# Base rows of a mixture-of-experts output: stored whole and overwritten, or added and scattered tile by tile

## The chip, the cores and the metric

The kernel runs on one core of one Trainium2 chip. The metric is the device time of one launch in microseconds; three runs of the kernel before gave a median of 1457.72 us. Times inside the kernel are from one profiled execution and count from the start of its span.

## What is computed

The input is 2048 tokens (2 x 1024) of 256 numbers. Four layers are applied one after another, each as `x = x + ffn(cond(x))`. The change lies in the end of the last one. Its `cond` part is a mixture of experts with a shared part: every token goes to two of eight experts, and the sum of shared and routed results is divided by three. Call its result h. Its `ffn` part is this, with 16 experts and room for 160 tokens in each:

```python
probs = softmax(h @ Wg)                          # 2048 x 16
top1_val, top1_idx = probs.max(-1), probs.argmax(-1)
masked = where(top1_idx[None, :] == arange(16)[:, None], top1_val[None, :], -inf)
vals, idx = top_k(masked, 160)                   # the best 160 tokens of each expert
y = gelu(h[idx] @ W1 + b1) @ W2 + b2
ffn = h.at[idx].set(y)                           # tokens without a place keep h
out = x + ffn
```

So a row of the output is x + y where the token has a place in its expert, and x + h, called the base row here, where it has none.

## The kernel before

Tokens are cut into 16 tiles of 128 (NT = 16, P = 128) and into four blocks of 512 (NB = 4). `k.Xt` holds x with one token in each of 128 partitions, 16 x 256 numbers wide; `k.Ht` (its tile is named ACC in the profile) holds h in the same way; `k.XT` and `k.HT` hold x and h with channels in the partitions, as TensorE needs them. SyncE (SP) issues the loads of weights and rows, ScalarE (ACT) a few stores, GpSimd (POOL) all transfers that go by a list of row numbers. A scheduler orders the instructions of each engine by their dependencies and by hints (`_behind` is such a hint: an order without a wait).

Layer 3 begins in `_cond_moe` (L1927) with the layer's `Last` object as `next`. Three blocks of the shared part are computed while the routing is worked out, then 39 expert slots, then the fourth block of the shared part. During this fourth block `Tokens.add` (L1656) loads two expert rows for each token (yt, 256 KB for a tile, five buffers) and VectorE adds them into Ht with their gates (L1665, two instructions for a tile). `_back` (L1584) transposes each finished tile into HT: TensorE writes ps_bk, ScalarE copies it (L1591).

The final routing, `Last.chunk` (L2206), works by block and is hooked into the same stretch:

- `logits` (L2216): ScalarE's queue stores h into the left half of the rows of a DRAM buffer hx (L2217); POOL adds h to x in place (L2219, 128x1024), so that Xt then holds the base rows; TensorE multiplies by Wg (l3f_pt), ScalarE copies.
- `top` (L2230): a transpose (l3f_pl), then VectorE takes the maximum (l3f_m, L2236), the difference (l3f_lg, L2238) and the choice (l3f_eq, L2241); ScalarE takes the exponential (L2242).
- `rows` (L2250): one-hot rows and the split gate value (l3f_z), multiplied by TensorE into l3f_ps (L2266); POOL keeps running counts (L2271 to L2273).
- `beats` (L2284): compares tokens with tokens to get each token's rank in its expert.

`Last.begin` (L2173) had, earlier, stored the old x into the right half of the rows of hx (L2190). `Last.finish` (L2323) runs what is left of the four blocks, issues the four stores of the base rows into the output (L2339 to L2343, 512 KB each, from SP), the 16 loads of b2 (into XT, which is free by then) and the first weights, and turns ranks into row numbers: `numbers` (L2396) makes, for each of 16 slots of 128 ranks and for 4 groups of 4 x 32 ranks, the list `src` of rows to gather and the list `dst` of rows to write. An empty place gets a number beyond the last row, and the transfer skips it (`bounds_check`). The b2 rows of the groups (b2g) go into the last four tiles of Ht (L2390).

`Last.run` (L2409) takes the 20 pieces in the order slot, slot, slot, slot, group and so on. Five gathers are begun ahead. For each piece TensorE transposes the gathered rows (ps_cm), VectorE copies them (xsT, L2484), TensorE multiplies by W1 (l3f_ph, or l3f_gh for a group), ScalarE applies gelu, TensorE multiplies by W2 (l3f_po), VectorE adds b2 and then x (ys, L2426 and L2427), and POOL scatters the 128 rows into the output (L2428). `_after(k, s, self.outs)` (L2433) makes the scatters wait until the four stores of base rows have landed. Then POOL issues the gather of the piece five places later (L2492).

Of the kernel before, what the change touches and what calls it, by code (L numbers as in the profile page):

```python
# [9 lines left out]
F32 = mybir.dt.float32  # L10
I32 = mybir.dt.int32
U32 = mybir.dt.uint32
# [1914 lines left out]
def _cond_moe(k, name, wr, bias, W1, W3, W2, nf, hold, R1, R2, gate_mult, final, lead, most, next=None):  # L1927

    nc, A, XT, HT, Xt, Ht = k.nc, k.A, k.XT, k.HT, k.Xt, k.Ht
    rp, pool, psum = k.rp, k.pool, k.psum  # L1930
    E, T, NS = 8, P, 39
    base = 0 if next else 8192
    w, rb = k.small[wr], k.small[bias]
    sets = []
    for i in range(4):
        r = k.ring.take(1, hold).rearrange("p (n c f) -> p n c f", n=2, f=D)
        sets.append([(r[:, 0], A[R1]), (r[:, 1], A[R2])])
    def routing(lead_):
        s = rp.tile([P, NT, E], F32, name=name + "_s", tag="s")
        _logits(k, psum, rp, XT, w, E, name, s, AF.Sigmoid, k.small[wr, "b"])  # L1940
        sel = rp.tile([P, NT, E], F32, name=name + "_sel", tag="lg")
        nc.vector.tensor_tensor(sel, s, _bc(rb, 1, [P, NT, E]), ALU.add)
        _, ixf = _top(nc, rp, sel, E, name)
        _name_rows(k, k.Xr, ixf, base)
        oh = [_one_hot(k, rp, ixf, n, E, name + "_oh%d" % n, "oh%d" % n) for n in range(2)]
        M = rp.tile([P, NT, E], F32, name=name + "_M", tag="M")
        nc.vector.tensor_add(M, oh[0], oh[1])
        cum = _running(k, rp, M, E, name)
        yield
        pos, eid, of, used = _route(k, rp, psum, M, cum, E, T, NS, len(sets), name)  # L1950
        rows = [_rows_of(k, rp, oh[n], pos, E, name + "_rows%d" % n, "rows%d" % n) for n in range(2)]
        k.x.begin()
        lead_.sends = k.x.paced(k.Xr, rows)

        nc.vector.tensor_mul(M, M, s)
        den = rp.tile([P, NT], F32, name=name + "_den", tag="den")
        nc.vector.tensor_reduce(den, M, AX.X, ALU.add)
        big = rp.tile([P, NT], F32, name=name + "_big", tag="big")
        nc.vector.tensor_single_scalar(big, den, 1e-9, ALU.is_gt)
        nc.vector.tensor_scalar_add(den, den, 1e-9)  # L1960
        nc.vector.reciprocal(den, den)
        nc.vector.tensor_mul(den, den, big)
        nc.vector.tensor_scalar(big, big, -0.5, 0.5, ALU.mult, ALU.add)
        gate = []
        for n in range(2):
            nc.vector.tensor_mul(oh[n], oh[n], s)
            g = rp.tile([P, NT], F32, name=name + "_g%d" % n, tag="g%d" % n)
            nc.vector.tensor_reduce(g, oh[n], AX.X, ALU.add)
            nc.vector.tensor_mul(g, g, den)
            nc.vector.tensor_add(g, g, big)  # L1970
            nc.vector.tensor_scalar_mul(g, g, gate_mult * final)
            gate.append(g)
        lead_.made = gate, eid, of, used

    def shared(tb, hook=None, mid=None, added=lambda: False):
        if nf == 8 and tb == 0:
            po = _shared_first(k, pool, psum, XT, W1, W3, W2, hook)
        else:
            po = _shared(k, pool, psum, XT, tb, W1, W3, W2, nf, hook, mid)
        for i in range(2):  # L1980
            t = tb * 4 + i * 2
            if added():
                nc.vector.scalar_tensor_tensor(Ht[:, t:t + 2, :], po[i], final, Ht[:, t:t + 2, :],
                                               ALU.mult, ALU.add)
            else:
                nc.scalar.activation(Ht[:, t:t + 2, :], po[i], AF.Copy, scale=final)

    lead_ = Lead(k, routing, *((1, 7), 2) if nf == 8 else ((1, 3), 4))
    def hook(f, mul, mm):
        if k.late and lead_.n >= 6:  # L1990
            k.late.pop(0)(mul)
        lead_.hook(f, mul, mm)

    for tb in range(lead):
        shared(tb, hook)
    gate, eid, of, used = lead_.finish()
    k.t.begin()
    by = Slots(k, pool, psum, of, base)

    def slots(lo, hi):  # L2000
        series = Series(k, by, lo, hi)
        for i in range(lo, hi):
            series.slot(i, _gelu_products(k, pool, psum), lambda: _slot_weights(k, eid, i, sets, E))
        series.close()

    used = nc.values_load(used[0:1, 0:1], min_val=0, max_val=NS)
    slots(0, most)
    with k.tc.If(used > most):  # L2008
        slots(most, NS)
    if next:  # L2010
        next.begin()
    c = Tokens(k, pool, psum, gate, Ht, HT, nf, next)
    for tb in range(lead, NB):
        c.there = tb * 4
        shared(tb, c.hook, c.hook, lambda: c.added >= tb * 4 + 4)
    c.there = NT
    k.ring.drop(hold)
    if next:
        next.finish(c)
    else:  # L2020
        c.finish()
# [104 lines left out]
class Last:  # L2126
# [10 lines left out]
    def __init__(self, k):  # L2137
        self.k, E = k, self.E
        rp = k.rp
        self.w = []  # L2140
        self.parts = [self.chunk(q) for q in range(NB)]

        self.plan = {5: [0], 6: [0], 7: [0, 1]}
        k.iota16 = rp.tile([P, CAP], BF16, name="iota16")
        k.nc.vector.tensor_copy(k.iota16, k.iota)
        k.one16 = rp.tile([P, 1], BF16, name="one16")
        k.nc.vector.memset(k.one16, 1.0)
        self.oh = rp.tile([P, NT, E], F32, name="l3f_oh")
        self.val = rp.tile([P, NT], F32, name="l3f_val")

        self.z = rp.tile([P, 4, 2, self.K], BF16, name="l3f_z")
        self.cum = rp.tile([P, NT + 1, E], F32, name="l3f_cum")

        self.acc = rp.tile([P, NT, 7], F32, name="l3f_acc")

        self.ids = rp.tile([P, NT, 2, E], BF16, name="l3f_ids")
        self.down = rp.tile([P, E], F32, name="l3f_down")
        self.th = rp.tile([P, NT], F32, name="l3f_th")
        self.outs = []

    def weights(self, ref=None):

# [10 lines left out]
    def begin(self):  # L2173
# [13 lines left out]
        nc.vector.memset(self.cum[:, 0, :], 0.0)  # L2187
        nc.vector.tensor_scalar(self.down, k.iota[:, 0:self.E], -1.0, float(self.E), ALU.mult, ALU.add)
        nc.vector.tensor_scalar_add(self.th, k.iota[:, 0:NT], 1.0)
        nc.sync.dma_start(k.hx[:, D:2 * D].rearrange("(t p) d -> p t d", p=P), k.Xt)  # L2190
        self.weights()

    def on_act(self, t):

# [11 lines left out]
    def chunk(self, q):  # L2206
# [8 lines left out]

        def logits(mul, mm):  # L2216
            nc.scalar.dma_start(k.hx[cols, 0:D].rearrange("(t p) d -> p t d", p=P), k.Ht[:, ts, :])  # L2217
            x = k.Xt[:, ts, :]
            nc.gpsimd.tensor_tensor(x, x, k.Ht[:, ts, :], ALU.add)  # L2219
            ps = psum.tile([P, P], F32, name="l3f_pt", tag="mm")  # L2220
            for c in range(2):
                for j in range(4):
# [100 lines left out]
    def finish(self, c):  # L2323
# [12 lines left out]
                    ref = p(None, None) or ref  # L2336
        ref = _warm(k, k.psum, ref, 6)
        assert c.put == NT
        for q in range(NB):  # L2339
            i = nc.sync.dma_start(k.out[q * TB:(q + 1) * TB, :].rearrange("(t p) d -> p t d", p=P),  # L2340
                                  k.Xt[:, 4 * q:4 * q + 4, :])
            _behind(k, i, c.load)
            self.outs.append(i.ins.name)  # L2343
        for e in range(E):
            i = nc.sync.dma_start(self.b2[:, e, :], k.A["L3_b2"][e:e + 1].to_broadcast([P, D]))
            _behind(k, i, c.load)
# [36 lines left out]
            _behind(k, i, ref)  # L2383
            ref = i
        self.ref = ref
        s, d, _ = self.numbers(pg, 4, "g")
        self.src, self.dst = ([t[:, i:i + 1] for t, n in ((a, E), (b, 4)) for i in range(n)]
                              for a, b in ((self.src, s), (self.dst, d)))

        self.b2g = k.Ht[:, 12:16, :]  # L2390
        for e in range(E):
            g = e % 4
            nc.sync.dma_start(self.b2g[32 * g:32 * g + 32, e // 4, :],
                              k.A["L3_b2"][e:e + 1].to_broadcast([32, D]))

    def numbers(self, ps, n, name):  # L2396
# [12 lines left out]
    def run(self):  # L2409
# [14 lines left out]
        def end(i, po, b2):  # L2424
            y = pool.tile([P, D], F32, name="ys", bufs=4)
            nc.vector.tensor_tensor(y, po, b2, ALU.add)  # L2426
            nc.vector.tensor_tensor(y, y, at[i][:, D:2 * D], ALU.add)  # L2427
            s = nc.gpsimd.indirect_dma_start(  # L2428
                out=k.out, out_offset=bass.IndirectOffsetOnAxis(ap=self.dst[i], axis=0),
                in_=y, in_offset=None, bounds_check=N - 1, oob_is_err=False)  # L2430
            k.tc.declare_no_dep(s.ins, group="out", reason="rows of their own")
            k.tc.add_to_no_dep_group("out", s.ins)
            _after(k, s, self.outs)  # L2433

        def slot(e, xT):
            W1, W2, _ = self.w[e]
# [45 lines left out]
        for n, i in enumerate(order):  # L2482
            xT = pool.tile([P, 2, P], F32, name="xsT", bufs=3)
            nc.vector.tensor_copy(xT, _channel_major(k, psum, at[i], self.ref))  # L2484
            if i < E:
                end(i, slot(i, xT), self.b2[:, i, :])
            else:
                end(i, group(i - E, xT), self.b2g[:, i - E, :])
                for e in range(4 * (i - E), 4 * (i - E) + 4):
                    k.ring.drop(self.w[e][2])  # L2490
                self.weights()
            fetch(n + 5)  # L2492


def _layer3(k):
# [127 lines left out]
```

## Time and profile before

| | |
|---|---|
| median of three runs | 1457.72 us (1453.08 to 1458.84) |
| profiled execution, own time | 1446.02 us |
| its span | 1444.3 us |
| PE busy | 1396.8 us, 97% of the span |
| VectorE busy | 464.0 us, 32% |
| ScalarE busy | 307.8 us, 21% |
| GpSimd busy | 291.5 us, 20% |
| first and last scatter into the output start | 1356.6 and 1437.2 us |
| granted TensorE clock, mean | 0.988 |

The table is from the page of the profile. A share of the span is a mean over stages that differ: most of the 1444 us are dense matrix products, while the end of layer 3, from about 1281 us on, is a chain of small steps on four engines and then the 20 pieces. PE, DVE, ACT, POOL and SP are TensorE, VectorE, ScalarE, GpSimd and SyncE. L2219 is line 2219 of the kernel before; `out<-in` names the tiles that an instruction writes and reads.

### The profile page before, as it was taken

How to read it: one execution, taken by the hardware profiler on the slowest of the kernel's cores; microseconds unless marked ns; L12 is line 12 of the kernel's file. 1: busy time of each engine (PE TensorE's matmuls, PEld its weight loads, DVE VectorE, ACT ScalarE, POOL GpSimd, SP SyncE). 2: the span in 40 equal slices, each digit the busy share in tenths (PEclk: the TensorE clock that was granted, in tenths of full speed). 3: DMA queues.
4: the chain of work that ended last, by engine and by line, in shares of the span. 5: the costliest groups of instructions: out<-in, count | busy, mean ns of one | idle time of the engine just before them, and what ended most of it. 6: DMA issues, size and time to landing. Idle time of an engine off the chain costs nothing. (4 is left out here: it accounts for less than half of the span.)

```text
span 1444.3 us, 23566 instructions
## 1 busy us (share of the span) xinstructions
PE 1396.8 (97%) x8606; PEld 1002.0 (69%) x8610; DVE 464.0 (32%) x1558; ACT 307.8 (21%) x646; POOL 291.5 (20%) x339
## 2 busy tenths in 40 slices
PE   9999999999999999999999999999999998997897
PEld 4544444545558865565999999999995567874675
DVE  4523322326214442511211111111115513467332
ACT  3222221234112121201111111111112211126221
POOL 0400001200533410331001001001010073433441
PEclk9999999999999999999999999999999999998999
DMA  9879994922314850421335155155507247758470
GB/s 313 297 256 347 358 321 134 275 72 101 125 52 118 260 183 8 188 82 37 113 109 194 48 180 195 46 178 194 193 20 273 93 164 244 225 172 284 123 243 15
DMA packets 176527, 246.78 MB, mean 171 GB/s; under 512 B 16695, under 2 KB 128831, under 8 KB 176400
## 3 DMA queue, kind: packets, MB, share of 16 engines
q1 hardware_dynamic: 154912, 203.18, 43.1%
q0 software_dynamic: 13888, 36.63, 7.2%
q10 hardware_dynamic: 7600, 5.34, 1.1%
q8 instruction: 72, 1.18, 0.3%
q14 instruction: 55, 0.45, 0.1%
HBM read 280.92 MB, written 47.22 MB: 227 GB/s over the span
## 5 line engine op out<-in xcount | busy, mean ns | idle before, releaser
L282 POOL DMA_INDIRECT tbuf<-ys,sdst x108 | 106.3, 984 | 484.8 <-ACT ys L1844 376.6
L1520 PE MATMUL spo<-ring,sa 128*128 128x256 f32 x704 | 164.9, 379 | 0.0
L1520 PEld LDWEIGHTS spo<-ring,sa 128*128 128x128 f32 x704 | 132.5, 190 | 44.6 <-issue 29.1
L1837 DVE TENSOR_TENSOR fa<-fsg,fpu 128x512 f32<-128x512 f32 x72 | 49.5, 688 | 316.2 <-PE fpu L1832 316.2
L1832 PE MATMUL fpg<-xsT,ring 128*128 128x128 f32 x1152 | 140.4, 275 | 0.7 <-issue 0.7
L1543 DVE TENSOR_TENSOR sa<-ssg,spu 128x512 f32<-128x512 f32 x88 | 60.4, 686 | 249.8 <-PE spu L1534 241.2
L1832 PE MATMUL fpu<-xsT,ring 128*128 128x128 f32 x1152 | 140.4, 275 | 0.0
L1832 PEld LDWEIGHTS fpg<-xsT,ring 128*128 128x128 f32 x1152 | 137.0, 192 | 2.7 <-issue 0.9
L1832 PEld LDWEIGHTS fpu<-xsT,ring 128*128 128x128 f32 x1152 | 134.4, 192 | 0.0
L1841 PE MATMUL fpo<-ring,fa 128*128 128x256 f32 x576 | 130.3, 379 | 0.0
L1841 PEld LDWEIGHTS fpo<-ring,fa 128*128 128x128 f32 x576 | 106.7, 190 | 13.0
L1539 ACT ACTIVATE ssg<-spg 128x512 f32<-128x512 f32 x88 | 52.6, 597 | 263.0 <-PE spg L1534 243.6
L1534 PE MATMUL spg<-HT,ring 128*128 128x512 f32 x192 | 92.1, 594 | 2.2 <-issue 1.9
L1534 PE MATMUL spu<-HT,ring 128*128 128x512 f32 x192 | 90.2, 592 | 0.0
L1808 PE MATMUL cph<-xsT,ring 128*128 128x128 f32 x576 | 79.0, 281 | 4.8 <-DMA ring<-in_L_r 2.6
L1836 ACT ACTIVATE fsg<-fpg 128x512 f32<-128x512 f32 x72 | 43.0, 597 | 171.7 <-PE fpg L1832 171.7
L1808 PEld LDWEIGHTS cph<-xsT,ring 128*128 128x128 f32 x576 | 71.2, 194 | 8.8 <-DVE sn L1735 2.8
L1534 PE MATMUL spg<-XT,ring 128*128 128x512 f32 x160 | 75.5, 593 | 1.3 <-PEq L2008 1.2
L1534 PE MATMUL spu<-XT,ring 128*128 128x512 f32 x160 | 75.2, 592 | 0.0
L1815 PE MATMUL cpo<-ring,ch 128*128 128x256 f32 x288 | 73.8, 380 | 0.0
L1534 PEld LDWEIGHTS spu<-HT,ring 128*128 128x128 f32 x192 | 36.3, 190 | 45.0 <-issue 44.2
L1731 DVE COPY xsT<-ps_cm 128x256 f32<-128x256 f32 x132 | 55.1, 418 | 36.7 <-PE ps_cm L365 36.5
(621 smaller groups left out, 1726.1 us busy)
## 6 DMA issues: line engine op xcount, KB each, us to landing
ring<-in_L_w SPq DMA_DIRECT2D x108, 1024.0 KB
ring<-in_L_r SPq DMA_DIRECT2D x72, 512.0 KB
ring<-in_L_r SPq DMA_DIRECT2D x144, 256.0 KB
xs<-xbuf SPq DMA_DIRECT2D x132, 129.0 KB
ring<-in_L_W SPq DMA_DIRECT2D x32, 512.0 KB
yt<-tbuf SPq DMA_DIRECT2D x48, 256.0 KB
XT<-in_L_r SPq DMA_DIRECT2D x16, 512.0 KB
HT<-in_L_r SPq DMA_DIRECT2D x8, 512.0 KB
```

The source lines that it names most:

```text
L282: i = k.nc.gpsimd.indirect_dma_start(out=self.ap, out_offset=bass.IndirectOffsetOnAxis(ap=idx, axis=0), in_=rows, in_offset=None, **end)
L1520: mm = nc.tensor.matmul(po[g // 2][:, g % 2, :], a[:, g * P:(g + 1) * P], W2[:, f, :], start=f == 0 and g % 2 == 0, stop=f == nf - 1, skip ...
L1534: mm = nc.tensor.matmul(ps, W[:, c, f * P:(f + 1) * P], X[:, c, cols], start=c == 0, stop=c == 1)
L1539: k.silu = nc.scalar.activation(sg, pg, AF.Silu)
L1543: mul = nc.vector.tensor_mul(a, sg, pu)
L1731: turned = nc.vector.tensor_copy(xT, _channel_major(k, self.psum, xs, made=made))
L1808: made = [nc.tensor.matmul(ph[:, f, :], R1[:, c, f * P:(f + 1) * P], xT[:, c, :], start=c == 0, stop=c == 1) for f in range(2) for c in ra ...
L1815: made = [nc.tensor.matmul(po, h[:, f, :], R2[:, f, :], start=f == 0, stop=f == 1) for f in range(2)]
L1832: made = [nc.tensor.matmul(ps[:, j, :], W[:, c, (f0 + j) * P:(f0 + j + 1) * P], xT[:, c, :], start=c == 0, stop=c == 1) for ps, W in ((pg, ...
L1836: nc.scalar.activation(sg, pg, AF.Silu)
L1837: nc.vector.tensor_mul(a[:, f0:f0 + 4, :], sg, pu)
L1841: made = [nc.tensor.matmul(po, a[:, f, :], W2[:, f, :], start=f == 0, stop=f == 4 * nh - 1) for f in range(4 * nh)]
```

## The change

The base rows are no longer stored as a whole. POOL's four additions into Xt and SP's four stores are gone, and with them the scatters' wait. Each token that has no place in its expert is found from its rank: `l3f_kept` is the token's own number if it has none, and a number beyond the last row if it has one. Beside pieces 1 to 16 VectorE adds one tile of 128 base rows, and POOL scatters it by this list, which skips the rows of routed tokens. Ht has to live until then, so b2g goes into two buffers of yt. The store of the old x into hx is moved in the text from `begin` to a hook in the first blocks of the shared part.

```diff
@@ _cond_moe, hook
         lead_.hook(f, mul, mm)
+        if next and lead_.n == 4:
+            next.base()
@@ Last.begin
-        nc.sync.dma_start(k.hx[:, D:2 * D].rearrange("(t p) d -> p t d", p=P), k.Xt)
         self.weights()
+
+    def base(self):
+
+        k = self.k
+        k.nc.sync.dma_start(k.hx[:, D:2 * D].rearrange("(t p) d -> p t d", p=P), k.Xt)
@@ Last.chunk, logits
             nc.scalar.dma_start(k.hx[cols, 0:D].rearrange("(t p) d -> p t d", p=P), k.Ht[:, ts, :])
-            x = k.Xt[:, ts, :]
-            nc.gpsimd.tensor_tensor(x, x, k.Ht[:, ts, :], ALU.add)
@@ Last.finish
-        for q in range(NB):
-            i = nc.sync.dma_start(k.out[q * TB:(q + 1) * TB, :].rearrange("(t p) d -> p t d", p=P),
-                                  k.Xt[:, 4 * q:4 * q + 4, :])
-            _behind(k, i, c.load)
-            self.outs.append(i.ins.name)
@@
-        s, d, _ = self.numbers(pg, 4, "g")
+        s, d, made = self.numbers(pg, 4, "g")
@@
-        self.b2g = k.Ht[:, 12:16, :]
+        away = k.rp.tile([P, NT], F32, name="l3f_away")
+        i = nc.vector.tensor_scalar(away, rank, 2.0 * CAP, 16384.0, ALU.is_lt, ALU.mult)
+        _behind(k, i, made)
+        self.kept = k.rp.tile([P, NT], U32, name="l3f_kept")
+        i = nc.vector.tensor_tensor(self.kept, away, k.tok, ALU.add)
+        _behind(k, i, made)
+
+        both = [k.pool.tile([P, 2, D], F32, name="yt", bufs=5) for _ in range(2)]
+        self.b2g = [both[i // 2][:, i % 2, :] for i in range(4)]
@@ Last.run
         def end(i, po, b2):
             y = pool.tile([P, D], F32, name="ys", bufs=4)
             nc.vector.tensor_tensor(y, po, b2, ALU.add)
-            nc.vector.tensor_tensor(y, y, at[i][:, D:2 * D], ALU.add)
+            made = nc.vector.tensor_tensor(y, y, at[i][:, D:2 * D], ALU.add)
+            put(y, self.dst[i])
+            return made
+
+        def put(y, to):
             s = nc.gpsimd.indirect_dma_start(
-                out=k.out, out_offset=bass.IndirectOffsetOnAxis(ap=self.dst[i], axis=0),
+                out=k.out, out_offset=bass.IndirectOffsetOnAxis(ap=to, axis=0),
                 in_=y, in_offset=None, bounds_check=N - 1, oob_is_err=False)
             k.tc.declare_no_dep(s.ins, group="out", reason="rows of their own")
             k.tc.add_to_no_dep_group("out", s.ins)
-            _after(k, s, self.outs)
+
+        def keep(t, ref):
+            x = k.Xt[:, t, :]
+            i = nc.vector.tensor_tensor(x, x, k.Ht[:, t, :], ALU.add)
+            _behind(k, i, ref)
+            put(x, self.kept[:, t:t + 1])
@@ the loop over the 20 pieces, n counts them
             fetch(n + 5)
+            if 0 < n <= NT:
+                keep(n - 1, made)
```

More of the change, by code (lines that the diff above doesn't have):

```diff
@@ L2158, in __init__ @@
         self.th = rp.tile([P, NT], F32, name="l3f_th")
-        self.outs = []
     def weights(self, ref=None):
@@ L2385, in finish @@
         self.ref = ref
-        s, d, _ = self.numbers(pg, 4, "g")
+        s, d, made = self.numbers(pg, 4, "g")
         self.src, self.dst = ([t[:, i:i + 1] for t, n in ((a, E), (b, 4)) for i in range(n)]
                               for a, b in ((self.src, s), (self.dst, d)))
-        self.b2g = k.Ht[:, 12:16, :]
+        away = k.rp.tile([P, NT], F32, name="l3f_away")
[6 more added lines that the diff above has]
+        self.b2g = [both[i // 2][:, i % 2, :] for i in range(4)]
         for e in range(E):
             g = e % 4
-            nc.sync.dma_start(self.b2g[32 * g:32 * g + 32, e // 4, :],
+            nc.sync.dma_start(self.b2g[e // 4][32 * g:32 * g + 32],
                               k.A["L3_b2"][e:e + 1].to_broadcast([32, D]))
@@ L2485, in run @@
             if i < E:
-                end(i, slot(i, xT), self.b2[:, i, :])
+                made = end(i, slot(i, xT), self.b2[:, i, :])
             else:
-                end(i, group(i - E, xT), self.b2g[:, i - E, :])
+                made = end(i, group(i - E, xT), self.b2g[i - E])
                 for e in range(4 * (i - E), 4 * (i - E) + 4):
```

## The prediction

> **What bounds the kernel now.** I began with the page: PE is busy 97% of the span, so a change pays only where PE waits or where the chain that ended last leaves PE. The change touches the last 160 us, so I read that chain there, in order of time:
>
> ```profile
> 1292.62 4.56 DVE ACC L1665 x7
> 1297.17 0.25 issue
> 1297.42 0.47 DVE ACC L1665
> 1297.90 0.60 DVE sa L1543
> 1298.49 1.59 DVE ACC L1665 x4
> 1300.08 0.14 DVE l3f_m L2236
> ...
> 1300.51 2.13 DVE l3f_eq L2241
> ```
>
> Before 1305 the chain is VectorE: the additions of the expert outputs into Ht (L1665), then the first steps of the final routing. One comparison on 64 columns takes 2.13 us there. The groups by tile and line say that this is not its price:
>
> ```profile
> L1665 DVE SCALAR_TENSOR_TENSOR ACC<-yt,l3c_g,ACC x32: 470/474/2596, 1284.0 to 1308.7; 128x256 f32<-128x256 f32 x32
> L2241 DVE TENSOR_SCALAR l3f_eq<-l3f_lg x4: 184/194/2120, 1300.5 to 1317.5; 128x64 f32<-128x64 f32 x4
> ```
>
> The columns are shortest/median/longest in ns. The timeline of GpSimd says who holds them:
>
> ```profile
> 1288.46 2.48 POOL L2219 TENSOR_TENSOR Xt<-Xt,ACC 128x1024 f32<-128x1024 f32 x1 [8.40 <-issue]
> 1294.34 2.48 POOL L2219 TENSOR_TENSOR Xt<-Xt,ACC 128x1024 f32<-128x1024 f32 x1 [3.40 <-DVE ACC L1665]
> 1300.22 2.35 POOL L2219 TENSOR_TENSOR Xt<-Xt,ACC 128x1024 f32<-128x1024 f32 x1 [3.40 <-DVE l3f_m L2236]
> ...
> 1309.32 2.36 POOL L2219 TENSOR_TENSOR Xt<-Xt,ACC 128x1024 f32<-128x1024 f32 x1 [3.90 <-DVE l3f_lg L2238]
> ```
>
> In the narrow windows the long instructions start at 1288.6 (2596 ns), 1294.5 (2585 ns) and 1300.5 (2120 ns), each just after one of these additions, and end with it. At the fourth, VectorE was waiting for PE. The reader sees three holds: 2.12 + 2.11 + 1.93 = 6.2 us of VectorE. Whether they are worth 6.2 us is asked of PE, in the busy time by stretch (PE first, granted clock after the five engines):
>
> ```profile
> 1285.00:1290.00 5.00, 5.00 (x19) 2.91 (x18) 4.83 (x9) 0.69 (x2) 1.54 (x1) 1.00 0.84 253
> 1290.00:1295.00 5.00, 5.00 (x20) 3.17 (x20) 5.00 (x10) 0.86 (x4) 1.60 (x2) 1.00 0.91 277
> 1295.00:1300.00 5.00, 5.00 (x40) 3.88 (x39) 5.00 (x8) 1.76 (x6) 1.82 (x1) 1.00 0.91 279
> 1300.00:1303.00 3.00, 1.62 (x9) 0.85 (x7) 2.86 (x6) 2.27 (x5) 2.35 (x1) 1.00 0.82 248
> ```
>
> PE works without a gap until 1300.9. Two of the three holds lie beside full PE.
>
> **Part 1: four additions leave POOL (L2218-2219).** Step by step, with the same instruction order on PE and ScalarE in both kernels:
> - Without the first two holds VectorE is 2.1 us early at 1291 and 4.2 us at 1297. But the last `sa` (L1543) needs spu, which PE ends at 1293.81 + 1.88 = 1295.7 whatever VectorE does. So `sa` runs 1295.7-1296.4, and the four L1665 behind it (1.67 us) end at 1298.1 instead of 1300.08. The yt loads may then hold it: loads 10 and 11 were issued at 1291.65 and 1292.06, when the held additions freed their buffers, and come earlier too. At 4.46 us to landing (the slowest in the chain) there is room.
> - l3f_m (L2236) needs the transpose l3f_pl, which PE ends at 1298.90 + 0.27 = 1299.17. It starts at 1299.2 instead of 1300.0: **0.8 us** of the 4.2 remain.
> - l3f_eq costs its 0.19 instead of 2.12: **1.9 us**.
> - What is late next is ScalarE. One L1665, ahead of the last l3f_z, needs the shared result copied by L1986. ScalarE's order is: store of hx, two copies (0.65), table load (1.28), Exp (0.26), two copies (0.65), L1986 (0.55). The first copies need PE's ps_bk, ended at 1299.06; the second pair needs the ps_bk after 1300.9. That puts L1986's first end near 1302.5, and VectorE is there at 1304.86 - 2.75 = 1302.1: **0.4 us given back**.
>
> PE's l3f_ps then starts near 1303.1 instead of 1305.52: 2.4 us. From there to 1347 the work passes between PE, VectorE and ScalarE one result at a time, so the lead is kept. The fourth addition held nobody: 0. If ScalarE gives nothing of its part early, the gain falls to 0; if PE's full stretch is itself loosened by VectorE, it is 6.2. I take 2.4, which is worked out from each engine's own rows.
>
> PE's clock adds an unknown: 0.89 granted in 1303-1308, 0.71 in 1308-1312, where 4 us at 0.71 lose 1.2 us. The gap ahead of it (1300.9 to 1305.5, with 1.4 us of transposes in it) gets shorter. I count 0 and keep 1.5 us on either side.
>
> **Part 2: four stores leave SP (L2339-2343), and what waited for them.** They took 0.37 to 0.46 us each to issue, and the fourth waited for its addition until 1311.71. So the b2 and weight loads behind them move up by some 4 us. Nobody waits there: the first ph at 1347.79 waits for xsT, and the eight weight loads were issued from 1317.19 to 1325. Scatters waited for the stores by semaphore: the first is at 1356.56, and the last store had landed by 1311.71 + 0.39 + 6.2 = 1318.3. 0 us, and 2 MB less to move.
>
> **Part 3: moved at no cost.** The store of Xt into hx has a new place in the text, but SP's order still has it between the layer-3 weight loads and `l3c_used`; it was issued at 1125.9 and reads as little as before. b2g goes to yt buffers, whose last reader is done by 1309.2, ahead of the issues from 1325; the first group reads it at 1373.63. l3f_away and l3f_kept are two steps of 0.17 us in the 2.00 us in which VectorE waits for the first ps_cm; without that cover they would cost 0.4.
>
> **Part 4: sixteen additions on VectorE.** The nearest row is L2427, also two SBUF tiles of 128x256: 424/425/426 ns, 20 times. 16 x 0.425 = 6.8 us. In VectorE's new order each follows its slot's two additions, and the xsT copy that PE needs next is behind it. After slot 1 the second addition ends at 1359.4 and xsT starts at 1359.85: 0.45 us of idle for 0.425. The other gaps ahead of xsT are 0.45, 1.33 or 1.34. And xsT itself is early: copied by 1360.6, first used by PE at 1361.94. So 0 us; with that cover gone it would be 6.8.
>
> The trace shows the neighbours of such an addition:
>
> ```profile
> 1397.29 0.97 POOL L338 DMA_INDIRECT HT<-hx,l3f_srcg  x1 [0.31 <-PE l3f_po L2450]
> 1398.10 0.42 DVE L2427 TENSOR_TENSOR ys<-ys,HT 128x256 f32<-128x256 f32 x1
> ```
>
> They overlap, and neither is longer than elsewhere. The Trainium skill speaks against this part ("SBUF — State Buffer", section "Who interferes with whom"): a VectorE instruction with two SBUF inputs contends with a GpSimd instruction that reads SBUF, and the later one blocks for the whole of the other. That is what L1665 shows beside L2219 (2596 against 474 ns). Applied to the sixteen additions beside POOL's index-driven DMAs it would hold each by up to one of them; the pair of rows above does not show it, and the measurement decides.
>
> **Part 5: sixteen scatters on POOL.** The nearest row is L2428: 982 to 1022 ns, and 0.30 us between two. 16 x 1.32 = 21 us. From 1356.56 to the end of the last scatter at 1438.14 there are 81.6 us; 20 scatters of 1.32 and 12 gathers of 1.27 fill 41.6, so 40.0 are free. In the tightest round, 1374.79 to 1395.96, 21.2 us hold five scatters and five gathers (12.95), and 8.2 are left for five new ones: 1.64 each. Queued behind each new scatter is a gather, five slots ahead. It comes up to some 3 us later; the gather of 1376.12 lands 3.6 us later at 1380.7, and PE reads it from 1389.75: 9 us of room. The last three slots have no such scatter, so the one at 1437.16 is not moved. 0 us. Not shown is a scatter most of whose rows are skipped: between 0 (it costs no more than its 1.32 on POOL) and the full 3.5 us of issue and landing (1.02 + 2.5) if POOL were held until it lands. I take 1.32: POOL issued the existing gathers without such a wait.
>
> **Sum.** 0.8 + 1.9 - 0.4 = 2.4 (2.36 before rounding). The profiled execution took 1446.02 us, its span 1444.3 with 1.7 around it: 1443.6, span 1441.9. The median of the three runs stands 11.7 above that execution, and they spread from 1453.08 to 1458.84. The difference is put on the median: 1457.7 - 2.4 = **1455.3**.
>
> **The rivals.**
> - *All of the hold comes back* (chance 0.18). For: the chain names L1665 throughout, and the shorter gap may spare PE its low clock. Against: PE has no gap until 1300.9. 1457.7 - 6.2 = 1451.5; with 1.5 of clock 1450.0.
> - *ScalarE takes over* (0.15): its table load and copies set the time of L1986 and the lead is lost. No change: 1457.7.
> - *Slower: POOL becomes the bound of the last slots* (0.12). Place: the new scatter ahead of the gathers and the next scatter. It decides from 40.0/16 = 2.5 us each. At the upper price of 3.5, 16 x (3.5 - 2.5) = 16 us late: 1457.7 - 2.4 + 16 = 1471. Against it stand the rows of L2428 and L338.
>
> The forecast has 0.55. The range takes in the first two rivals and the clock, 1450 to 1460; the slower case is left out. Faster or slower by over 0.5%, 7.3 us, is about what a measurement of this kernel can tell from no change. Faster: 0.16 (the first rival with clock, and the spread of the runs on the forecast). Slower: 0.12. Between: 0.72.
>
> **What would show it.** L1665 without an instruction over 0.5 us, l3f_eq four times near 0.19, l3f_ps 2.4 us earlier against the end of the last spo; POOL with 16 more DMAs near 1 us and its last scatter still set by the last ys; the new additions at 0.42 us and no gap of PE ahead of l3f_ph in the last slots. Wrong I would be if the scatters of skipped rows passed 1.6 us, if the additions were held, or if PE's clock fell elsewhere.

## The result, and the profile after

The changed kernel is slower: 1473.7 us, median of five runs (1468.69 to 1474.66), beside 1458.6 us for the kernel before (1453.08 to 1462.07); ratio 1.0099, 95% interval 1.0070 to 1.0128. That is 15 us where 2.4 us less was forecast. Its profiled execution took 1474.66 us, span 1472.9. Measured again beside the kernel before on three more chips, the ratio was 1.0075 (1.0060 to 1.0090), 1.0080 (1.0067 to 1.0093) and 1.0070 (1.0057 to 1.0083).

**The routing went as forecast.** Groups by line, after (shortest/median/longest in ns; line 2244 was 2241, line 2446 is the new addition):

```profile
L1665 DVE SCALAR_TENSOR_TENSOR ACC<-yt,l3c_g,ACC x32: 474/481/487, 1298.8 to 1320.5; 128x256 f32<-128x256 f32 x32
L2244 DVE TENSOR_SCALAR l3f_eq<-l3f_lg x4: 184/192/196, 1314.5 to 1330.1; 128x64 f32<-128x64 f32 x4
L2446 DVE TENSOR_TENSOR Xt<-Xt,ACC x16: 418/419/420, 1371.5 to 1450.9; 128x256 f32<-128x256 f32 x16
```

No L1665 is longer than 487 ns and no l3f_eq longer than 196: the holds are gone, and none of the sixteen additions is held. The chain in order of time, after:

```profile
1311.52 1.92 PE spo L1520 x8
1313.44 0.23 PE ps_bk L1588 x2
...
1313.70 0.65 ACT HT L1591 x2
...
1314.36 1.28 ACT L2245
...
1317.18 0.48 DVE ACC L1665
...
1317.82 0.62 PE l3f_ps L2269 x8
```

Where VectorE's additions stood before, the chain is now PE's last spo, then ScalarE's copies and its table load (L2245), with one addition.

**The time is lost in the last slots.** From the first to the last xsT the 20 pieces take 93.2 us instead of 77.7, and GpSimd is not what they wait for: its scatters take 0.98 to 1.02 us and wait for ys. The timeline of after, around the tenth piece:

```profile
1396.38 2.62 PE L2455 MATMUL l3f_ph<-xsT,ring 128*128 128x128 f32 x22
...
1396.65 0.99 POOL L2438 DMA_INDIRECT out<-Xt,l3f_kept  x1 [0.31 <-issue]
...
1397.95 0.99 POOL L338 DMA_INDIRECT HT<-hx,l3f_src  x1 [0.30 <-issue]
1399.25 1.01 POOL L2438 DMA_INDIRECT out<-ys,l3f_dst  x1 [0.30 <-issue]
1400.56 0.99 POOL L2438 DMA_INDIRECT out<-Xt,l3f_kept  x1 [0.30 <-issue]
1401.51 1.14 ACT L2461 ACTIVATE l3f_h<-l3f_ph,w_b 128x128 f32<-128x128 f32 x4 [6.25 <-remote]
1401.86 0.99 POOL L338 DMA_INDIRECT HT<-hx,l3f_srcg  x1 [0.30 <-issue]
...
1401.93 3.52 PE L2465 MATMUL l3f_po<-ring,l3f_h 128*128 128x256 f32 x8 [2.94 <-issue]
```

And the same piece before:

```profile
1379.88 2.62 PE L2440 MATMUL l3f_ph<-xsT,ring 128*128 128x128 f32 x22
...
1381.24 1.02 POOL L2428 DMA_INDIRECT out<-ys,l3f_dst  x1 [1.33 <-DVE ys L2427]
1381.92 1.14 ACT L2446 ACTIVATE l3f_h<-l3f_ph,w_b 128x128 f32<-128x128 f32 x4 [3.15 <-PE l3f_ph L2440]
1382.34 1.99 PE L2450 MATMUL l3f_po<-ring,l3f_h 128*128 128x256 f32 x8
```

Before, ScalarE starts gelu 2.04 us after PE began ph. After, it is 5.13 us, though PE's record is the same 2.62 us: PE's result reaches ScalarE 3.1 us late ("remote" means that the trace has no record of the signal that ended the wait). Meanwhile GpSimd issues one indirect transfer after another with only 0.30 us between them. PE then runs at a lower clock (0.55 granted from 1401.9 to 1405.5) and takes 3.52 us for eight matmuls instead of 1.99.

There is a second difference, upstream. The trace of after has a gap of 13 us in PE at 1177 to 1190 us, far from the change, and the trace of before that the prediction rests on has none. So both kernels were run again first.

### The profile page after: what moved, and what is told of

The parts are those of the page before. It is cut to its first block, busy times and chain, and to the rows that moved or that the text cites. A ratio compares the mean times of both kernels' runs of the same rounds, so it can differ in the third digit from the quotient of the medians.

```text
span 1472.9 us, 23612 instructions
## 1 busy us (share of the span) xinstructions
PE 1403.2 (95%) x8606; PEld 1005.9 (68%) x8610; DVE 464.3 (32%) x1576; ACT 307.5 (21%) x646; POOL 297.9 (20%) x351
## 5 line engine op out<-in xcount | busy, mean ns | idle before, releaser
L1520 PE MATMUL spo<-ring,sa 128*128 128x256 f32 x704 | 168.6, 385 | 15.6 <-DVE sa L1543 15.6
```

The costliest lines, as they stand in the source:

```text
L1520: mm = nc.tensor.matmul(po[g // 2][:, g % 2, :], a[:, g * P:(g + 1) * P], W2[:, f, :], start=f == 0 and g % 2 == 0, stop=f == nf - 1, skip ...
```

## The experiments

Two theories at the start. **A**: the sixteen scatters delay what others wait for in the last slots. **B**: such waits come and go with the execution, not with the change. Rivals inside A followed: rows that are written, a fuller GpSimd queue, a share for each scatter, or a row of indirect transfers without a pause (called R).

| run | kernel | median, us | kernel before beside it | ratio (95%) |
|---|---|---|---|---|
| a1 | after again | 1470.3 | 1458.9 | 1.0075 (1.0060 to 1.0090) |
| a2 | before again | 1459.7 | 1458.9 | 1.0000 (0.9989 to 1.0012) |
| a3 | after, no scatters | 1456.9 | 1458.9 | 0.9981 (0.9969 to 0.9993) |
| a4 | before, plus scatters | 1479.2 | 1458.9 | 1.0141 (1.0120 to 1.0161) |
| b1 | after, no row moved | 1469.0 | 1457.5 | 1.0077 (1.0064 to 1.0091) |
| b2 | after, memsets for scatters | 1455.5 | 1457.5 | 0.9987 (0.9979 to 0.9996) |
| b3 | after, eight scatters | 1463.3 | 1457.5 | 1.0035 (1.0022 to 1.0048) |
| b4 | before, additions on VectorE | 1454.6 | 1457.5 | 0.9978 (0.9969 to 0.9987) |
| c1 | after, scatters spaced | 1446.6 | 1448.0 | 0.9995 (0.9983 to 1.0007) |
| c2 | b4, three in a row upstream | 1444.4 | 1448.0 | 0.9973 (0.9963 to 0.9983) |
| d1 | after | 1470.9 | 1457.9 | 1.0080 (1.0067 to 1.0093) |
| d2 | as c1 | 1458.9 | 1457.9 | 1.0012 (0.9999 to 1.0025) |
| d3 | as c2 | 1460.5 | 1457.9 | 1.0010 (0.9998 to 1.0022) |
| d4 | as b4 | 1456.3 | 1457.9 | 0.9989 (0.9979 to 1.0000) |
| e1 | b4, short pauses upstream | 1451.4 | 1447.2 | 1.0027 (1.0018 to 1.0037) |
| e2 | b4, long pauses upstream | 1458.0 | 1447.2 | 1.0068 (1.0050 to 1.0085) |
| f1 | after | 1469.4 | 1458.9 | 1.0070 (1.0057 to 1.0083) |
| f2 | as e1 | 1453.4 | 1458.9 | 0.9974 (0.9955 to 0.9992) |

Each letter is one chip. On the chips of c and e the kernel before takes 1447 to 1448 us and no trace shows a late result; on the other four it takes 1458 to 1459 us, and all their traces show late results upstream, beside a row of seventeen or more scatters.

### a1 and a2: both kernels again, unedited

> The changed kernel once more, unedited, for a second trace of it. In its first trace two stretches are longer than in the trace of before: one wait of VectorE at L1543 (15.5 us, until 1189 us, where PE's record of its matmuls had ended 15 us earlier) and the last slots (93.2 us from first to last xsT against 77.7 us before). Theory A (the sixteen scatters delay others in the last slots): the last slots are about 93 us again, and the long wait at 1175-1189 need not come back. Theory B (the long waits come and go with the execution, not with the change): the last slots are some other length, between 78 and 93 us, and the sum differs. Time 1469 to 1475 us by both.

> The kernel before once more, unedited, for a second trace of it: the first was of an execution of 1446.0 us, 12 us under the median of 1457.7 us. By both theories the time is 1453 to 1462 us. Theory A: the last slots are 77.7 us again, within 1 us, and the missing 12 us stand elsewhere. Theory B: late results like those of the changed kernel appear in this kernel's last slots or upstream, for some 12 us in all.

The last slots: 92.8 us in a1 and 78.0 in a2, as theory A has it. But a2, the kernel before, has the wait upstream as well. There PE computes the shared part: ScalarE makes ssg of PE's result spg, VectorE makes sa of ssg and PE's spu, and PE's next product, spo, needs sa. The timeline of a2:

```profile
1172.84 1.89 PE L1520 MATMUL spo<-ring,sa 128*128 128x256 f32 x8
...
1182.00 0.96 POOL L282 DMA_INDIRECT xbuf<-Xt,l3c_rows  x1 [0.30 <-issue]
1186.23 0.60 ACT L1539 ACTIVATE ssg<-spg 128x512 f32<-128x512 f32 x1 [19.22 <-remote]
1186.86 0.69 DVE L1543 TENSOR_TENSOR sa<-ssg,spu 128x512 f32<-128x512 f32 x1 [16.80 <-ACT ssg L1539]
...
1187.61 0.79 PE L1520 MATMUL spo<-ring,sa 128*128 128x256 f32 x1 [12.88 <-DVE sa L1543]
```

GpSimd issues the scatters into xbuf twenty in a row here, from 1157.83 to 1182.96. PE's records end at 1174.7, but ScalarE gets the result only 3.3 us after the last of the twenty. Nobody waits for instructions here: from 1170 to 1187 us no packet of an instruction queue moves in this trace. So the wait upstream belongs to neither kernel. It would explain why the first profiled execution of before (1446.0 us) stood 11.7 us under its median: its trace lacks this wait, like those of the chips of c and e. Theory A holds for the last slots. B holds for the upstream wait in so far as the change does not bring it; but it goes with the chip rather than with the execution: the kernel before took 1454.7 us or more in every run on the chips of a, b, d and f, and 1452.0 us or less in every run on those of c and e. Which chip the first execution of before ran on is not recorded.

### a3 and a4: the scatters taken away, and added to the kernel before

```diff
 a3, on the changed kernel
             _behind(k, i, ref)
-            put(x, self.kept[:, t:t + 1])
 a4, on the kernel before (l3f_away and l3f_kept made as in the changed kernel)
             fetch(n + 5)
+            if 0 < n <= NT:
+                put(k.Xt[:, n - 1, :], self.kept[:, n - 1:n])
```

> The changed kernel without the sixteen scatters of base rows; the sixteen additions on VectorE stay. Rows of the output that are not routed are not written. Theory A (scatters): the last slots come back to 78 us, and the time to 1455 us or a little less, -15 us to -18 us against the changed kernel. Rival (the additions, or the parts ahead of the last slots, carry the loss): 1468 to 1474 us as with them.

> The kernel before with sixteen scatters of base rows added after the slots, as in the changed kernel, of rows that the four stores have written already; stores and the additions on GpSimd stay, nothing is added on VectorE but the two short steps for the row numbers. Theory A (scatters): the last slots grow by 15 us, and the time to 1470 to 1475 us. Rival (the additions on VectorE, or the parts ahead of the last slots): 1454 to 1462 us, as before.

Without the scatters 13.4 us go (1470.3 to 1456.9) and the last slots take 78.1 us: the additions cost nothing, and what is left is 2.0 us under the kernel before. With them added to the kernel before, 20.3 us come. Nothing holds them back there, so GpSimd runs sixteen in a row, the eight gathers at the head of the last slots among them. Timeline of a4, at the end of this row:

```profile
1366.43 1.89 PE L2460 MATMUL l3f_po<-ring,l3f_h 128*128 128x256 f32 x8
...
1368.16 1.50 PE L2450 MATMUL l3f_ph<-xsT,ring 128*128 128x128 f32 x12
...
1374.70 0.99 POOL L2438 DMA_INDIRECT out<-Xt,l3f_kept  x1 [0.30 <-issue]
1378.32 0.42 DVE L2433 TENSOR_TENSOR ys<-l3f_po,XT 128x256 f32<-128x256 f32 x1 [11.03 <-remote]
1378.40 1.14 ACT L2456 ACTIVATE l3f_h<-l3f_ph,w_b 128x128 f32<-128x128 f32 x4 [13.21 <-remote]
...
1378.82 3.78 PE L2460 MATMUL l3f_po<-ring,l3f_h 128*128 128x256 f32 x8 [9.15 <-ACT l3f_h L2456]
```

VectorE waits for po and ScalarE for ph, two results whose records ended at 1368.3 and 1369.7. Both start within 0.1 us of each other, 2.6 us after the end of the row (1375.69). This wait and a second one, beside a row of fourteen, hold 17 us of the loss; the later pieces lose nothing, when GpSimd has sent its sixteen.

### b1 and b2: what it is about a scatter

```diff
 b1
-        i = nc.vector.tensor_scalar(away, rank, 2.0 * CAP, 16384.0, ALU.is_lt, ALU.mult)
+        i = nc.vector.tensor_scalar(away, rank, 1.0e9, 16384.0, ALU.is_lt, ALU.mult)
 b2
-            put(x, self.kept[:, t:t + 1])
+            for _ in range(4):
+                nc.gpsimd.memset(k.Ht[:, t, :], 0.0)
```

> The changed kernel with every row number of l3f_kept out of bounds, so that the sixteen scatters are issued and move no row (rows that are not routed are not written). Theory P (what delays PE's results is GpSimd issuing indirect transfers one after another): 1470 to 1474 us, the last slots about 93 us from first to last xsT, as with rows. Theory D (it is the rows that are written, 768 packets in the last slots): 1456 to 1458 us and 78 us, as without the scatters.

> The changed kernel with each scatter of base rows replaced by four memsets on GpSimd of the dead tile of Ht, some 1.0 to 1.3 us in all (rows that are not routed are not written). If a GpSimd queue that is merely fuller delays the gathers or the last scatters: 1470 to 1474 us. If it takes indirect transfers (P or D): 1456 to 1459 us, the last slots 78 us.

Scatters that move no row cost as much (ratio 1.0077); memsets in their place cost nothing (0.9987, last slots 78.6 us). It is neither the rows nor a busy GpSimd, but the indirect transfer itself. One thing in the expectation of b1 was misread: the 768 packets are not the rows. The DMA lines of b1 and of a3 for the last slots (packets, MB, share):

```profile
q0 software_dynamic: 3328, 7.14, 20.4%
```

```profile
q0 software_dynamic: 2559, 7.13, 21.6%
```

Each scatter brings 48 packets though it moves nothing. So b1 does not separate GpSimd's issuing from these packets.

### b3, c1 and d2: fewer scatters, and the same ones spaced out

```diff
 b3
-            put(x, self.kept[:, t:t + 1])
+            if t % 2 == 0:
+                put(x, self.kept[:, t:t + 1])
 c1, d2 (kept starts at 0)
-            if 0 < n <= NT:
-                keep(n - 1, made)
+            for _ in range({2: 1, 3: 2, 6: 1, 8: 2, 12: 2, 13: 3, 14: 1, 15: 1, 16: 2, 18: 1}.get(n, 0)):
+                keep(kept, made)
+                kept += 1
```

> The changed kernel with eight of the sixteen scatters, those of even tiles (rows of odd tiles that are not routed are not written). If each scatter costs its share, half of the 13 to 17 us remain: 1463 to 1466 us. If the loss needs a long run of indirect transfers without a pause on GpSimd (the traces show PE's results arriving late only in such runs of seven and more), it is nearly gone: 1456 to 1459 us.

> The changed kernel with all its sixteen scatters and additions, but put where GpSimd has time to spare in the last slots (one or two behind pieces 2, 3, 6, 8, 12, three behind 13, then 14, 15, 16, 18), so that GpSimd issues at most four or five indirect transfers without a pause instead of nine. Theory R (PE's results arrive late where indirect transfers are issued without a pause): most of the loss goes, 1456 to 1460 us, the last slots 78 to 81 us. Share theory (each scatter costs its share of the 14 us, wherever it stands): 1469 to 1474 us, about 92 us.

> The changed kernel, unedited, beside d2, d3 and d4 on one chip. In the call of c1 and c2 the kernel before took 1448 us, 10 us under all its earlier runs, and no result of PE came late in their traces: that chip does not show the late results, so that c1 had no kernel beside it that loses. If this chip shows them (before near 1458 us): 1469 to 1474 us, a ratio of 1.0075 to 1.010. If it does not (before near 1448 us): theory R expects 1444 to 1448 us, nothing lost at all; if the scatters cost their share by themselves, 1457 us or more there too.

> The sixteen scatters where GpSimd has time to spare, as c1. If this chip shows late results: theory R 1456 to 1460 us, the last slots 78 to 81 us; share theory 1469 to 1474 us. If it does not: like c1, a ratio of 0.9995, and d1 tells whether spacing had anything to mend.

Half of the scatters keep half of the loss: 7.8 us over b2. Alone that speaks for a share of each, against what R expected; but its trace still has rows of seven (with one pause of 0.53 us in it) and eight transfers, and its two largest losses (4.5 and 2.5 us over a3) lie at them. c1 landed on a chip without late results and decides nothing. d1 and d2 decide: the same sixteen scatters and additions cost 1470.9 us as the change has them and 1458.9 us where GpSimd has time to spare. Twelve of thirteen microseconds went with the placing alone, so the share theory is out. Timeline of d2 for GpSimd at the place shown above:

```profile
1390.22 0.99 POOL L338 DMA_INDIRECT HT<-hx,l3f_src  x1 [0.31 <-issue]
1393.23 1.01 POOL L2438 DMA_INDIRECT out<-ys,l3f_dst  x1 [2.03 <-DVE ys L2433]
1394.55 0.99 POOL L2438 DMA_INDIRECT out<-Xt,l3f_kept  x1 [0.30 <-issue]
1395.84 0.99 POOL L338 DMA_INDIRECT HT<-hx,l3f_srcg  x1 [0.30 <-issue]
1397.14 1.01 POOL L2438 DMA_INDIRECT out<-ys,l3f_dst  x1 [0.30 <-DVE ys L2433]
1398.45 1.00 POOL L338 DMA_INDIRECT HT<-hx,l3f_src  x1 [0.30 <-PE l3f_po L2465]
1401.61 1.27 POOL L2438 DMA_INDIRECT out<-ys,l3f_dst  x1 [2.17 <-DVE ys L2433]
```

A pause of 2 us (the bracket is idle time) stands before and after these five; in a1 and d1 nine follow one another here. Behind the eight gathers that open the last slots, d2 has no row of more than five. The last slots take 80.6 us.

### b4 and d4: the gain without the scatters

The four stores stay, but later; the additions leave GpSimd for VectorE's idle time at the head of the last slots, the first behind the row numbers (`made`) and three behind the first xsT. b2g goes to yt buffers as in the change:

```diff
-            nc.gpsimd.tensor_tensor(x, x, k.Ht[:, ts, :], ALU.add)
...
-        for q in range(NB):
-            i = nc.sync.dma_start(k.out[q * TB:(q + 1) * TB, :].rearrange("(t p) d -> p t d", p=P),
-                                  k.Xt[:, 4 * q:4 * q + 4, :])
...
+        def base(q, ref=None):
+            ts = slice(4 * q, 4 * q + 4)
+            x = k.Xt[:, ts, :]
+            i = nc.vector.tensor_tensor(x, x, k.Ht[:, ts, :], ALU.add)
+            if ref is not None:
+                _behind(k, i, ref)
+            i = nc.sync.dma_start(k.out[q * TB:(q + 1) * TB, :].rearrange("(t p) d -> p t d", p=P), x)
...
         for n in range(5):
             fetch(n)
+        base(0, self.made)
         for n, i in enumerate(order):
...
+            if n == 0:
+                for q in range(1, NB):
+                    base(q, made)
```

> The kernel before with its four stores kept, and its four additions moved off GpSimd to VectorE's free time at the head of the last slots (one behind the row numbers, three behind the first xsT), stores behind them; no scatter of base rows. By both theories there is no row of indirect transfers more than in the kernel before, so the gain of 2.0 us without the additions on GpSimd stays: 1455 to 1458 us, a ratio of 0.998. If three additions of some 1.4 us hold the second xsT, or the first scatter waits for the stores and the gathers with it: up to 3 us more, 1459 to 1461 us.

> The kernel of b4 once more, beside d3. If this chip shows late results: 1454 to 1457 us with the wait at 1170 to 1189 us, a ratio of 0.998. If it does not: 1444 to 1446 us.

0.9978 and 0.9989: 2.9 and 1.6 us faster than the kernel before, and faster than the change by 14 us (d4 beside d1). The four additions take 1.2 us each, and the last slots 78.1 and 78.2 us. This version is faster than the change clear of noise, and faster than the kernel before in b4; the interval of d4 just reaches 1.0000.

### c2, d3, e1, e2 and f2: the wait upstream

If R is right, the wait upstream must go when its twenty scatters into xbuf get pauses. In c2 and d3 they were to follow VectorE's steps three at a time; in e1, e2 and f2 a memset stands behind each:

```diff
 c2, d3, on b4
-    lead_ = Lead(k, routing, *((1, 7), 2) if nf == 8 else ((1, 3), 4))
+    lead_ = Lead(k, routing, *((1, 7), 2) if nf == 8 else ((1, 3), 3))
 e1, f2, on b4, in Rows.scatter; for layer 3 k.x.pause is a tile of 128x256 (e2: 128x512)
+        if self.pause is not None:
+            if self.last is not None:
+                _behind(k, i, self.last)
+            self.last = i
+            self.last = k.nc.gpsimd.memset(self.pause, 0.0)
+            _behind(k, self.last, i)
```

> The kernel of b4 (additions on VectorE, four stores) with one number changed far from the last slots: GpSimd sends three of the thirty-two scatters into xbuf (L282) behind each step of VectorE instead of four, so that there is a pause of some 1.4 us after every three. In all second traces PE's results arrive 13 to 18 us late there, at 1166 to 1189 us, in both kernels. Theory R: that wait goes and the time falls to 1443 to 1450 us; the last scatters leave up to 3 us later, which is counted in. Rival (the late results at that place have another cause, and only lie beside the scatters): 1454 to 1459 us as without the pacing, or up to 5 us more for the later scatters.

> Three scatters into xbuf behind each step of VectorE instead of four, on top of d4, as c2. If this chip shows late results: theory R 1443 to 1450 us, without the wait of 13 to 15 us at 1170 to 1189 us; rival 1454 to 1459 us. If it does not: the same as d4 within 3 us (1442 to 1447 us).

> The kernel of b4 with a memset of 128x256 on GpSimd behind each of the thirty-two scatters into xbuf (L282) of layer 3, some 0.3 us each, so that no two of them are issued with less than about 0.6 us between them; d3's pacing had left seventeen in a row. Theory R (PE's results come late where indirect transfers are issued one after another): the wait of PE of 13 to 15 us at 1170 to 1189 us goes; the scatters end near where they do now (1205 us) and PE waits for the first slot's rows instead, so 1446 to 1454 us. Rival (the wait there has another cause): it stays, 1455 to 1460 us.

> As e1 with memsets of 128x512, some 0.5 us each. Theory R: no late result at 1170 us either, and the scatters end some 6 us later than in e1, which PE waits for: 1450 to 1460 us. If the pause of e1 is too short, the wait is there in e1 and gone or shorter here. Rival: the wait stays in both, 1458 to 1468 us.

> The changed kernel, unedited, beside f2. If before takes some 1448 us here (a chip without late results, as for c1, c2, e1 and e2): theory R, for which the chip has to bring the late results, expects nothing lost, 1444 to 1449 us and last slots of 78 us; if the dense scatters cost by themselves: 1455 us or more. If before takes some 1458 us: 1469 to 1474 us, as three times before.

> The kernel of e1 again. If before takes some 1458 us here: theory R has no wait at 1170 to 1189 us and 1450 to 1456 us; the rival has the wait and 1458 to 1466 us. If before takes some 1448 us: 1451 us as in e1, and the cause of that wait stays argued and not shown.

c2, e1 and e2 ran where there is no late result, and show only what pacing costs: c2 nothing (0.9973, like b4), e1 4.2 us more than the kernel before, e2 10.8. d3 missed: its pacing left seventeen in a row, since GpSimd started late and had steps to catch up on. But the run ended 3.8 us sooner after its start than the run of twenty (21.3 us against 25.1), and PE's gap fell from 12.9 to 8.8 us. In sum d3 is still 4.2 us slower than d4: its last slots begin 2.4 us later and, with a row of seven where d4 has five, take 80.5 us against 78.2. f2 says more. Busy time by stretch (length, then PE, PEld, DVE, ACT, POOL; behind these the granted clock), d4 first, without pauses:

```profile
1170.00:1180.00 10.00, 4.72 (x15) 2.48 (x14) 0.69 (x1) 0.00 (x0) 7.56 (x9) 0.92 0.39 140
1180.00:1190.00 10.00, 2.36 (x6) 1.91 (x7) 0.69 (x1) 0.84 (x2) 4.11 (x5) 0.50 0.16 55
```

f2, a memset of 0.33 us behind each scatter, on another chip with late results:

```profile
1170.00:1180.00 10.00, 10.00 (x33) 5.79 (x32) 1.10 (x2) 1.79 (x3) 8.84 (x15) 1.00 0.26 94
1180.00:1190.00 10.00, 10.00 (x32) 5.70 (x30) 0.69 (x1) 0.83 (x2) 8.84 (x15) 1.00 0.26 93
1190.00:1200.00 10.00, 4.25 (x17) 2.87 (x16) 1.38 (x2) 0.97 (x3) 8.84 (x15) 1.00 0.25 92
```

With the pauses PE works without a gap through the stretch in which d4 waits. All other traces of the four chips have that wait, d3 with its seventeen in a row too, and in the nine of a, d and f ScalarE resumes 3.0 to 3.5 us after the last transfer of the row. But results still come late in f2. Its timeline:

```profile
1181.51 1.88 PE L1541 MATMUL spg<-XT,ring 128*128 128x512 f32 x4
...
1189.76 0.60 ACT L1546 ACTIVATE ssg<-spg 128x512 f32<-128x512 f32 x1 [8.13 <-PE spg L1541]
1192.02 1.99 PE L1527 MATMUL spo<-ring,sa 128*128 128x256 f32 x8 [1.75 <-issue]
...
1204.39 1.12 PE L372 MATMUL ps_cm<-ident,xs 128*128 128x128 f32 x4 [5.93 <-DMA xs<-xbuf]
```

And the same step in e1, the same kernel on a chip without late results:

```profile
1181.74 1.88 PE L1541 MATMUL spg<-XT,ring 128*128 128x512 f32 x4
...
1183.66 0.60 ACT L1546 ACTIVATE ssg<-spg 128x512 f32<-128x512 f32 x1 [4.56 <-PE spg L1541]
```

ScalarE takes up spg 1.92 us after PE began it in e1 and 8.25 us after in f2: 6.3 us late. The spg before this one is 2.8 us late, and d4's, with no pauses, 15.0 (16.88 us). So 0.49 us between two transfers (the memset and 0.16 us of idle time) makes the lateness smaller and does not end it. PE had other matmuls to do until 1190; then it waits 1.75 and 2.45 us for late results and 5.93 us for the first slot's rows, which the pauses move back, while b4 and d4 have no wait there. From 1190 to 1210 PE is busy for 9.7 us, against 20 in d4. So f2 trades one wait for others and in sum (0.9974) is no better than b4 (0.9978). That dense rows of indirect transfers bring the late results is shown in the last slots, by placing (d2); upstream the lateness shrinks when they are spread (f2), as R has it, but the expectation that no result is late with these pauses failed. A kernel that gains from pauses here was not found.

## Why the prediction was wrong

The forecast was 2.4 us faster within 1450 to 1460; measured was 15 us slower, and 10 to 13 us slower in the repetitions (1470.3 against 1458.9 in a). By its steps, with a1 and a2, which ran on the same chip:

- **Part 1 held.** From the first spg of the last quarter to l3f_m it is 0.53 us earlier (0.8 forecast), l3f_eq falls from 2118 to 196 ns (1.92; 1.9 forecast), 0.18 us come back to l3f_ps (0.4 forecast): l3f_ps is 2.26 us earlier, for 2.36. ScalarE's copies and table load are late next, as said. The lead is kept to the first gather (3.09 us), and a3, the change without its scatters, is 2.0 us faster by the medians. Both rivals about this part, all of the hold or none of it, fall.
- **Parts 2 and 3 held**: nothing in a3 waits for the stores or the moved loads.
- **Part 4 held.** The sixteen additions took 418 to 420 ns (0.425 forecast) and cost nothing in a3. The Trainium skill's rule ("SBUF — State Buffer", section "Who interferes with whom") describes L1665 beside the GpSimd addition; in these runs no addition was held by an indirect transfer.
- **Part 5 is the step that failed**: "0 us" for the sixteen scatters, measured 13.4 (a1 less a3). Its arithmetic of GpSimd was right: 0.98 to 1.02 us each, and the last scatter waits for the last ys. What the step asked, whether GpSimd has the time, was the wrong question. The 40 us that it counted as free were the pauses between indirect transfers; once the scatters fill them, PE's results come late, 3.1 us at the piece shown in the trace of after and 4.5 to 6.3 us at the same piece in a1, d1 and f1. The last slots, first gather to last scatter, take 94.4 us in a2, 109.2 in a1 and 94.4 in a3.
- **The slower rival** had the size (1471) but not the cause, so that its size came out is chance: GpSimd did not become the bound, no scatter came near 3.5 us, and b2 shows that a GpSimd busy with memsets costs nothing.
- **The sign that was there.** The profiled execution stood 11.7 us under the median, and the prediction carried that as a constant. a2 shows what it very likely was: a gap of 12.9 us in PE beside twenty indirect transfers without a pause. The trace that was read lacked the very wait that the change adds more of; of the executions behind the median there is no trace, but they took as long as those of a2.

Open stays why a result is late. Either PE's last matmuls end later than their modelled records, or the signal of a finished PE is held up. The granted clock speaks for the second, though it does not prove it: in d4 PE's records end at 1174.7, the clock is 0.60 from 1178 to 1180 and 0.50 after, and ScalarE goes on only at 1186.3. In e1, where PE waits for rows and no result is late, the records end at 1194.0 and the clock is 0.74 from 1196 to 1198 and 0.50 after. So the clock falls about as soon after PE's last record in both, as if PE had ended when its records say, some 7 us before ScalarE learns of it in d4.

Open is also how dense a row must be. The eight gathers at the head of the last slots follow one another without a pause in a2 as well, and the first result beside them is not late: gelu starts 3.91 us after PE began ph, 3.82 in c1. f2 has late results with pauses of 0.49 us. Nor does b1 separate GpSimd's issuing from the 48 packets of each scatter. All traces with late results, f2's too, also lack some records of PE's signals (1135 to 1179, against 1268 or 1269 in the traces without), so the recording itself may take part; this rival was not tried, and every timed run here comes with a recorded span and clock. And the change itself was not run on a chip without late results; c1, its spaced form, is level with the kernel before there (0.9995).

## What to carry to other kernels

Idle time of GpSimd is not free for indirect transfers: look in its timeline for how many follow one another with only their 0.3 us between, and put new ones where it pauses (in rows of at most five, d2 cost 2.6 us over d4 for sixteen; as the change has them, d1 cost 14.6), or use plain stores, as b4 does. Whether it matters depends on the chip: on two of six nothing was late. When an execution that is profiled lies well under the median, find out what the others wait for before costing a change by its trace.

## What the runs showed of the hardware

- On four of six chips, PE's results reach ScalarE and VectorE 3 to 15 us late during a row of indirect transfers from GpSimd, and 3.0 to 3.5 us after its end where the row is seventeen or twenty long (a, d, f); with a memset of 0.33 us between every two transfers the lateness falls from 15.0 (d4) to at most 6.3 us (f2). On two chips (c, e) no trace shows it, and the kernel before takes 1447 to 1448 us instead of 1458.
- An indirect scatter that moves no row still takes GpSimd 1 us and brings 48 packets.
- After such a wait PE is slow as well: eight matmuls of 128x256 take 3.5 to 3.8 us instead of 1.9 to 2.0, at a granted clock of 0.55 in after (1401.9 to 1405.5) and 0.50 in a4 (1378 to 1382).
